# Sorting the 21-slot block inside the round instead of at its end, reading rows back later, and finishing the last three rounds side by side

## The chip, the core and the metric

The kernel runs on one core of a Trainium2 chip. The metric is the device time of one execution in microseconds (us); the number given for a kernel is the median of its timed runs. Engines are called by the profile's names: PE (TensorE matmuls), PEld (its weight loads), DVE (VectorE), ACT (ScalarE), POOL (GpSimd) and SP (SyncE). [...]

## What is computed

The input is 16 graphs of 1024 nodes with 64 features, an adjacency of 16 x 1024 x 1024 and a node mask. Four layers follow each other, each one `layernorm(x + layer(x))`. Layers 0 and 1 are dense message passing. Layers 2 and 3 are what the changed code does: for every node and feature, the values of the neighbours are sorted and weighted quantiles are taken, then a small MLP follows.

```python
adj_d = _dilate_adj(adj, mask)                        # thins out long neighbour lists
vals  = jnp.where(valid[..., None], x[:, None, :, :], big)
sv    = jnp.sort(vals, axis=2)                        # per node and feature, over neighbours
for tau, wt in zip((.25, .5, .75), (.25, .5, .25)):   # lo, hi: floor and ceil of tau * (m - 1)
    agg = agg + wt * (gather(lo) * (1.0 - frac) + gather(hi) * frac)
h = relu((x + agg) @ W1 + b1);  y = (h @ W2 + b2) * mask
```

## The kernel before

**Tiles and slots.** The 1024 nodes of a graph are ordered by the length of their neighbour list and cut into 8 blocks of 128 rows. A block is sorted as a dense list of a fixed number of slots, 64 features in each: `SIZES = (10, 11, 13, 14, 15, 17, 19, 21, 33)`. Blocks 0 to 6 (the "listed" classes t0 to t6, with 10 to 19 slots) have all their rows' neighbours fetched by POOL: one indirect DMA a slot and graph (line 378, tile `got_s`), from a table of the layer's features in DRAM. The last block is split in two halves of 64 rows; one graph's half needs up to 21 slots, the other's up to 33, and two graphs' halves are put side by side on the 128 partitions. So each pair of graphs has a block of class t7 (21 slots) and one of class t8 (33 slots). They aren't fetched: `fill` picks their values with one-hot matrices on PE (line 374, 24 matmuls for one slot of one graph, called a pick here), into PSUM tile `pgk`, and ACT copies them to SBUF tile `got` (line 780). The one-hots (`hot`) are made by DVE, every fourth by ACT.

**Rounds.** The 16 graphs are 8 pairs and there are two sorting layers, so 16 rounds (layer, pair), k0 to k15: (0,0), (0,1), (1,0), (0,2), (1,1), (0,3), ..., (0,7), (1,6), (1,7). `sort_round(k)` goes through t6, t5, ..., t0 for both graphs at once, then t7, then t8. `exchange` runs the min/max network of a class on DVE (49 instructions for t7, 66 for t8, 222 for t0 to t6); `weigh` multiplies the wanted slots on ACT and adds them on DVE. `finish` does the MLP and the layernorm, and POOL writes the rows by an indirect DMA (line 888): to the output, or to the table of the next layer, from which `read_back` loads them with an SP DMA (line 902) and splits them into three bf16 parts for `fill`.

**The ring.** `got_s` has `ROOM = 60` slots for both graphs of a round, the classes of a round need 99. `fetch` lets POOL go ahead as far as slots are free: t6, t5 and t4 of a round take slots 0 to 50, and t3 takes slots 0 to 13 again, so t3's gathers wait until t6 of their own round is sorted and weighed.

**The order of the work.** All instruction streams of DVE, ACT and PE are written out by generators that `Weave` runs by an estimated DVE clock: each `yield n` says that n us of DVE work should come before the generator goes on, and `catch_up` is called after each exchange instruction. So the preparation of later graphs (`features`, `lists`, `ordered`), `fill`, `weigh` and `finish` lie between the exchanges in an order fixed when the program is built. `weave.finish(gen)` and `weave.advance` write out a generator's rest at once.

The functions that the change touches are `fill` (line 762), `read_back` (line 897), `finish_round` (line 1018) and `sort_round` (line 1038). In `fill` the loop runs over the graphs, and within a graph over slots 1 to 32; `filled[layer]` of a graph is set when its 32 picks are out, and `read_back` of graph b waits for `filled[1]` of graph b - 2. At its end `sort_round` does this:

```python
        weave.finish(filling)
        for t in range(LISTED, NS):
            off = sum(SIZES[LISTED:t])
            got = tails[k][:, off : off + SIZES[t], :]
            other = s.lists.tile([P, WIDE, C], F32, name="other", bufs=1)
            exchange(t, (got, other[:, : SIZES[t], :]), cut)
            summed(t, got, None, (0, 1))
```

Of the kernel before, what the change touches and what calls it, by code (L numbers as in the profile page):

```python
# [12 lines left out]
F32 = mybir.dt.float32  # L13
# [8 lines left out]
P = 128  # L22
# [5 lines left out]
LISTED = 7  # L28
# [188 lines left out]
def adj_resnorm_kernel(ctx: ExitStack, tc: tile.TileContext, x, adj_t, nodemask, w01, b01, w02, b02,  # L217
# [49 lines left out]
    def halves_of(b):  # L267

        return (7, 8) if b % 2 == 0 else (8, 7)
# [100 lines left out]
    def pick(dst, hot, parts, first=True):  # L370

        for c in range(NT):
            for q in range(3):
                nc.tensor.matmul(dst, hot[:, c, :], parts[:, c, q, :], start=first and c + q == 0,  # L374
                                 stop=c == NT - 1 and q == 2)
# [386 lines left out]
    def fill(k):  # L762

        while k and (k - 1, NS - 1) not in free:
            yield 1
        size, short = SIZES[NS - 1], SIZES[NS - 2]
        got = tails[k] = s.lists.tile([P, short + size, C], F32, name="got", tag="got_l", bufs=1)
        layer, both = members(k)
        for m, b, e in both:
            while e.parts[layer] is None or e.xs[layer] is None or e.place is None or e.none is None:  # L770
                yield 1
            at = [(rows, (0, short)[plan - LISTED], SIZES[plan]) for rows, plan in zip((lower, upper), halves_of(b))]
            for rows, off, _ in at:
                nc.scalar.copy(got[rows, off, :], e.xs[layer][rows, NT - 1, :])
            waiting = None

            def empty():
                for rows, off, most in at:
                    if waiting[0] < most:
                        nc.scalar.copy(got[rows, off + waiting[0] : off + waiting[0] + 4, :], waiting[1][rows])  # L780

            for i in range(1, size):
                if i % 4 == 1:
                    first, pg = i, pgs[i // 4 % 2]
                if i % 4 == 1:

                    far = s.work.tile([P, NT, P], F16, name="far", bufs=1)
                    nc.scalar.activation(far, e.place, AF.Abs, bias=minus_k[:, i + 2 : i + 3])
                    by_act = s.lists.tile([P, NT, P], BF, name="hot", bufs=HOTS)
                    nc.scalar.activation(by_act, far, AF.Relu, bias=one_f, scale=-1.0)  # L790
                if i % 4 == 3:
                    hot = by_act
                else:
                    hot = s.lists.tile([P, NT, P], BF, name="hot", bufs=HOTS)
                    dve.tensor_scalar(hot, e.place, float(i), None, op0=ALU.is_equal)
                whole = i < LEAST[NS - 2]
                if not whole:
                    nc.tensor.matmul(pg[:, i - first, :], e.none,
                                     ident_b[: KW - 1, i - 1 : i].to_broadcast([KW - 1, C]), start=True, stop=False)
                pick(pg[:, i - first, :], hot, e.parts[layer], whole)  # L800
                yield 2.4
                if i % 4 == 2 and waiting:
                    empty()
                if i % 4 == 0:
                    waiting = first, pg
            yield 5
            empty()
            yield 0.5
            e.filled[layer] = True

    def weigh(k, t, got, agg, which, present):

# [84 lines left out]
    def read_back(b, e, src):  # L897

        while b >= 2 and not entries[b - 2].filled[1]:
            yield 2  # L900
        x3 = s.feat.tile([P, NT, C], F32, name="x3", bufs=1)
        nc.sync.dma_start(x3, src[:N, :].rearrange("(t p) c -> p t c", p=P))
        yield 60
        parts = s.feat.tile([P, NT, 3, C], BF, name="x3p", bufs=2)
        yield from split(x3, parts, x3)
        e.parts[1] = parts
# [40 lines left out]
    entries = [SimpleNamespace(near=None, taken=False, packed=False, listed=False, there=None, place=None, none=None,  # L947
                               wts=None, parts=[None, None], xs=[None, None], filled=[False, False], ends=None) for _ in range(B)]
    weave = Weave()
    tails = {}  # L950
    free, gots, room, holders = set(), [], [0], [None] * ROOM
    allowed, fetched = [1], [0, 0]
    order_of_rounds = [(0, 0), (0, 1)]
# [23 lines left out]
    def fetch(must=-1):  # L977

        moved = True
        while moved:  # L980
            moved = False
            for m in range(2):
                n = fetched[m]
                if n < len(tasks) and (m == 0 or n <= fetched[0]):
                    moved = fetch_one(n, m, must) or moved
# [32 lines left out]
    def finish_round(k, agg, sums):  # L1018
        for gen in sums:
            while weave.runs(gen):  # L1020
                yield 1
        layer, both = members(k)
        if k == len(order_of_rounds) - 1:
            for m, b, e in both:
                weave.add(finish(b, e, layer, agg[:, m], m == 1))
            return
        for m, b, e in both:
            yield from finish(b, e, layer, agg[:, m])

    def exchange(t, pair, view):  # L1030

        for is_max, d, v, i, j, to in usual[t]:
            dve.tensor_tensor(view(pair[to], v, d if is_max else 0), view(pair[i], v), view(pair[j], v, d),
                              op=ALU.max if is_max else ALU.min)
            weave.catch_up()
            fetch()

    def sort_round(k):

        if k >= 2:  # L1040
            weave.finish(rounds[k - 2])
        filling = weave.add(fill(k), 4.0, 0.7 if k < 3 else 1.0)
        agg = s.feat.tile([P, 2, NT, C], F32, name="agg")
        sums = []

        def summed(t, got, which, present):
            if len(sums) >= 2:
                weave.finish(sums[-2])
            sums.append(weave.add(weigh(k, t, got, agg, which, present)))
            weave.catch_up()  # L1050

        for n, (_, t, present) in enumerate(tasks):
            if tasks[n][0] != k:
                continue
            fetch(n)
            got = gots[n]
            which = slice(present[0], present[-1] + 1)
            count = len(present)
            other = s.lists.tile([P, WIDE, C], F32, name="other", bufs=1)
            other = other[:, : count * SIZES[t], :].rearrange("p (e s) c -> p e s c", e=count)  # L1060
            exchange(t, (got[:, which], other), cut_pair)
            summed(t, got, which, present)
        weave.finish(filling)
        for t in range(LISTED, NS):
            off = sum(SIZES[LISTED:t])
            got = tails[k][:, off : off + SIZES[t], :]
            other = s.lists.tile([P, WIDE, C], F32, name="other", bufs=1)
            exchange(t, (got, other[:, : SIZES[t], :]), cut)
            summed(t, got, None, (0, 1))
        if k:  # L1070
            weave.finish(rounds[k - 1])
        rounds.append(weave.add(finish_round(k, agg, sums)))
# [308 lines left out]
```

## Time and profile before

| | |
|---|---|
| timed runs | 7385.34, 7337.73, 7328.73 us; median 7337.73 us |
| the profiled execution | 5306.79 us, its span 5304.9 us |
| DVE busy | 4297.6 us, 81% of the span |
| POOL busy | 3464.7 us, 65% |
| PE busy | 3435.2 us, 65%; weight loads 2659.3 us, 50% |
| ACT busy | 2809.1 us, 53% |
| mean granted PE clock | 0.743 |
| POOL's indirect DMAs | 2944 gathers, 128 + 128 row writes |

The profiled execution took 2031 us less than the median of the timed runs; the page is of the profiled one. A busy share is a mean over the whole span, in which the first rounds, the middle and the last rounds have different limits. In a wait line the first number is the total, then how many times, then the longest. A wait is that of the engine named first[...]. DVE's groups are all recorded at line 211, a helper, so they are told apart by tiles.

### The profile page before, as it was taken

The numbers are of one execution on the slowest core, as the hardware profiler recorded it, in microseconds if no ns is written. First come the engines' busy times: TensorE is split into PE (matmuls) and PEld (weight loads), VectorE is DVE, ScalarE is ACT, GpSimd is POOL, SyncE is SP. The second block draws the span as 40 slices with busy tenths as digits, with TensorE's granted clock in tenths as the row PEclk, the third lists the DMA queues.
The fourth block names the chain that finished last, engine by engine and source line by source line (L and its number), as shares of the span: only waits on it lengthen the run. The fifth ranks groups of instructions, "written<-read, shape, count | busy, mean of one in ns | idle before, by whom it ended". The sixth has DMA issues, their size and how long they took to land. (4 is left out here: it accounts for less than half of the span.)

```text
span 5304.9 us, 109613 instructions
## 1 busy us (share of the span) xinstructions
PE 3435.2 (65%) x43576; PEld 2659.3 (50%) x43576; DVE 4297.6 (81%) x9266; ACT 2809.1 (53%) x6314; POOL 3464.7 (65%) x3296
## 2 busy tenths in 40 slices
PE   6878886385775776666776785777769563424152
PEld 5756555264554565555565563655547352324141
DVE  2577849698788989797997988798999999596775
ACT  3466465456564665737384563738475653334242
POOL 0336417757567776767767574776767777777771
PEclk7888787687877787868787786878887775555555
DMA  2212212222222222222212122222222111111110
GB/s 84 76 50 69 68 32 66 47 48 54 48 60 52 59 61 57 57 55 45 73 41 58 46 52 53 57 59 50 60 50 58 25 28 26 25 24 27 26 24 7
DMA packets 420617, 259.31 MB, mean 49 GB/s; under 512 B 106602, under 2 KB 368890, under 8 KB 420090
## 3 DMA queue, kind: packets, MB, share of 16 engines
q0 software_dynamic: 102400, 105.06, 10.4%
q1 hardware_dynamic: 317690, 147.12, 9.7%
q8 instruction: 343, 5.62, 0.5%
q14 instruction: 184, 1.51, 0.1%
HBM read 239.37 MB, written 12.59 MB: 47 GB/s over the span
## 5 line engine op out<-in xcount | busy, mean ns | idle before, releaser
L378 POOL DMA_INDIRECT got_s<-table,idx x2944 | 3170.9, 1077 | 1650.7 <-issue 604.9
L374 PEld LDWEIGHTS <-hot 128*128 128x128 bf16 x24576 | 972.2, 109 | 1011.9 <-DVE hot L211 696.7
L374 PE MATMUL pgk<-x3p,hot 128*128 128x64 bf16 x12288 | 544.0, 211 | 460.8 <-DVE hot L211 396.6
L211 DVE TENSOR_TENSOR other<-got_s 128x512 f32<-128x512 f32 (+9 forms) x850 | 508.7, 609 | 387.4 <-DMA got_s<-table,idx 352.9
L374 PE MATMUL pgk<-x2p,hot 128*128 128x64 bf16 x12288 | 525.5, 208 | 320.4 <-DVE hot L211 261.6
L780 ACT COPY got<-pgk 64x256 f32<-64x256 f32 x416 | 151.6, 365 | 675.8 <-PE pgk L374 670.3
L536 PE MATMUL pr<-steps,near 128*128 128x512 bf16 x1536 | 415.1, 431 | 131.6 <-ACT junk L542 84.6
L211 DVE TENSOR_TENSOR got_s<-got_s 128x128 f32<-128x128 f32 (+9 forms) x867 | 482.0, 560 | 17.8
L481 PE MATMUL pa<-x,adj_r 128*128 128x65 f32 x2048 | 391.3, 375 | 133.7 <-ACT x L404 58.6
L628 PE MATMUL pk<-near,order 128*128 128x512 f16 x2048 | 468.0, 382 | 4.5 <-DVE order L211 4.2
L829 ACT ACTIVATE got_s<-got_s,wts 128x64 f32<-128x64 f32 x1568 | 396.5, 335 | 135.1 <-DVE got_s L211 128.9
L481 PEld LDWEIGHTS pa<-x,adj_r 128*128 128x128 f32 x2048 | 380.6, 289 | 141.7 <-ACT x L404 60.5
L211 DVE TENSOR_TENSOR got_s<-other 128x512 f32<-128x512 f32 (+9 forms) x731 | 402.2, 563 | 7.5
L211 DVE TENSOR_SCALAR hot<-place 128x1024 bf16<-128x1024 f16 x768 | 329.8, 435 | 60.1 <-PE pgk L374 60.0
L536 PEld LDWEIGHTS <-near 128*128 128x128 f16 x1536 | 162.2, 109 | 353.0 <-issue 228.4
L211 DVE TENSOR_TENSOR other<-other 128x384 f32<-128x384 f32 (+10 forms) x617 | 324.0, 525 | 17.3
L211 DVE MAX8 best<-code 128x8 f16<-128x1024 f16 x240 | 293.9, 1225 | 48.1 <-ACT code L639 43.0
L628 PEld LDWEIGHTS <-order 128*128 128x128 bf16 x2048 | 194.0, 98 | 233.6 <-issue 10.6
L542 ACT ACTIVATE junk<-pr,nb_st 128x1024 f16<-128x1024 f32 x256 | 281.7, 1105 | 36.7 <-PE pr L536 35.9
L580 PE MATMUL pv<-minus_n,takes 128*128 128x128 bf16 x1024 | 212.5, 241 | 133.1 <-DVE takes L211 132.6
L790 ACT ACTIVATE hot<-far,one_f 128x1024 bf16<-128x1024 f16 x256 | 294.0, 1148 | 8.6
L450 PE MATMUL px<-adj_r,x_s 128*64 128x128 f32 x2048 | 287.9, 302 | 13.6 <-ACT node_in L453 9.2
(205 smaller groups left out, 6748.9 us busy)
## 6 DMA issues: line engine op xcount, KB each, us to landing
adj_r<-in_adj_dram SPq DMA_DIRECT2D x256, 512.0 KB
got_s<-table,idx POOLq DMA_INDIRECT x2944
x_s<-in_x_dram SPq DMA_DIRECT2D x16, 256.0 KB
table<-x SPq DMA_DIRECT2D x16, 256.0 KB
x<-table SPq DMA_DIRECT2D x16, 256.0 KB
table<-x3s,rows POOLq DMA_INDIRECT x128
out_dram<-agg,out_rows POOLq DMA_INDIRECT x128
table<-no_row SPq DMA_DIRECT2D x12, 0.2 KB
```

Source lines behind the costliest of these rows:

```text
L211: return call(*args, **kwargs)
L374: nc.tensor.matmul(dst, hot[:, c, :], parts[:, c, q, :], start=first and c + q == 0, stop=c == NT - 1 and q == 2)
L378: nc.gpsimd.indirect_dma_start(out=dst, out_offset=None, in_=tab, in_offset=bass.IndirectOffsetOnAxis(ap=rows, axis=0))
L450: nc.tensor.matmul(px[C:, q * P : (q + 1) * P], x_s[:, jt, :], adj[t][:, jt, :], start=jt == 0, stop=jt == NT - 1)
L481: nc.tensor.matmul(pa[:, q, :], adj[i][:, jt, :], x1[:, jt, :], start=jt == 0, stop=jt == NT - 1)
L536: nc.tensor.matmul(pr[:, h * HALF : (h + 1) * HALF], near[:, c, t * P : (t + 1) * P], steps[:, ONSET + h * HALF - c * P :][:, :HALF], star ...
L542: nc.scalar.activation(junk, prs[t - 1], AF.Sign, bias=lim[:, i, t - 1 : t], scale=-1.0, accum_out=cut_at[:, i, t - 1 : t])
L580: nc.tensor.matmul(pv[:, cols], takes[:, c, rows], minus_n, start=False, stop=False)
L628: nc.tensor.matmul(cols, order[:, c, t * P : (t + 1) * P], left(c, slice(h * G, (h + 1) * G)), start=c == 0, stop=c == NT - 1)
L780: nc.scalar.copy(got[rows, off + waiting[0] : off + waiting[0] + 4, :], waiting[1][rows])
L790: nc.scalar.activation(by_act, far, AF.Relu, bias=one_f, scale=-1.0)
L829: nc.scalar.activation(got[:, m, i, :], got[:, m, slot_id, :], AF.Copy, scale=e.wts[:, t, i : i + 1])
```

## The change

- `fill` keeps two tiles, `got_21` and `got_33`, where it had one of 54 slots, and turns its loops round: slots 1 to 20 of both graphs first, then slots 21 to 32 of both. A mark (k, 1) is set when the first part is out. `filled[layer]` of a graph is set at the end of its second part.
- `sort_round` sorts t7 ahead of t1 (after t2), once the mark (k, 1) is there; in the first round, k0, it stays at the end. t8 stays at the end.
- `read_back` of graphs 0 to 11 issues its SP DMA 60 us of DVE clock later, and the split comes 40 us after that, where it was 60 us after an immediate DMA. Graphs 12 to 15 stay as they were.
- `finish_round` lets the two graphs of rounds k13, k14 and k15 finish side by side (the second one in the buffers of `features` and in two other PSUM banks); before, only k15 did this, and the others finished one graph after the other.

```diff
 def fill(k):
-        size, short = SIZES[NS - 1], SIZES[NS - 2]
-        got = tails[k] = s.lists.tile([P, short + size, C], F32, name="got", tag="got_l", bufs=1)
+        middle, most = SIZES[NS - 2], SIZES[NS - 1]
+        ends = [s.lists.tile([P, size, C], F32, name="got", tag=f"got_{size}", bufs=1) for size in (middle, most)]
+        tails[k] = ends
         layer, both = members(k)
-        for m, b, e in both:
+        groups = 0
+        for low, high in ((1, middle), (middle, most)):
+            for m, b, e in both:
...
-            for i in range(1, size):
+                for i in range(low, high):
...
-            yield 5
-            empty()
-            yield 0.5
-            e.filled[layer] = True
+                yield 5
+                empty()
+                yield 0.5
+                if high == most:
+                    e.filled[layer] = True
+            filled.add((k, low))
 def read_back(b, e, src):
         while b >= 2 and not entries[b - 2].filled[1]:
             yield 2
+        if b < B - 4:
+            yield 60
         x3 = s.feat.tile([P, NT, C], F32, name="x3", bufs=1)
         nc.sync.dma_start(x3, src[:N, :].rearrange("(t p) c -> p t c", p=P))
-        yield 60
+        yield 60 if b >= B - 4 else 40
 def finish_round(k, agg, sums):
-        if k == len(order_of_rounds) - 1:
+        if k < order_of_rounds.index((0, B // 2 - 1)):
             for m, b, e in both:
-                weave.add(finish(b, e, layer, agg[:, m], m == 1))
-            return
-        for m, b, e in both:
-            yield from finish(b, e, layer, agg[:, m])
+                yield from finish(b, e, layer, agg[:, m])
+        else:
+            ends = [weave.add(finish(b, e, layer, agg[:, m], m == 1)) for m, b, e in both]
+            while any(weave.runs(gen) for gen in ends):
+                yield 1
 def sort_round(k):
+        def end(t):
+            got = tails[k][t - LISTED]
+            other = s.lists.tile([P, WIDE, C], F32, name="other", bufs=1)
+            exchange(t, (got, other[:, : SIZES[t], :]), cut)
+            summed(t, got, None, (0, 1))
+
         for n, (_, t, present) in enumerate(tasks):
...
+            if t == 1 and len(present) == 2:
+                while (k, 1) not in filled:
+                    weave.advance()
+                end(NS - 2)
             fetch(n)
...
         weave.finish(filling)
-        for t in range(LISTED, NS):
-            ...
+        if k == 0:
+            end(NS - 2)
+        end(NS - 1)
```

## The prediction

> **What bounds the kernel now.** I read the page first, then DVE's and POOL's waits, the timelines of round k7, SP's waits, and last the windows of the end.
>
> ```profile
> span 5304.9 us, 109613 instructions
> ...
> PE 3435.2 (65%) x43576; PEld 2659.3 (50%) x43576; DVE 4297.6 (81%) x9266; ACT 2809.1 (53%) x6314; POOL 3464.7 (65%) x3296
> ...
> DVE  2577849698788989797997988798999999596775
> ...
> POOL 0336417757567776767767574776767777777771
> ```
>
> DVE is the fullest engine, near nine tenths in the middle of the span. But a share doesn't say what it waits for. DVE's waits over the whole span, then (second fence) from 961 to 3745 us alone, which holds k1's t1 to k10's t1:
>
> ```profile
> DVE other L211 <- DMA got_s<-table,idx: 352.9, 28, 26.4
> DVE hot L211 <- PE pgk L374: 60.0, 28, 5.4
> ...
> DVE near L211 <- DMA adj_r<-in_adj_dram: 36.0, 7, 22.6
> ```
> ```profile
> DVE other L211 <- DMA got_s<-table,idx: 188.9, 14, 26.4
> ...
> DVE near L211 <- DMA adj_r<-in_adj_dram: 22.6, 1, 22.6
> ```
>
> One wait towers: exchanges whose gathered rows haven't landed. In the timeline of DVE in k7 it is one hole, between the end of t2 and the first exchange of t1; POOL's timeline of the same round shows why.
>
> ```profile
> 2787.02 0.42 DVE L211 TENSOR_TENSOR y_x<-pd,x_s 128x256 f32<-128x256 f32 x1
> 2812.33 0.56 DVE L211 TENSOR_TENSOR other<-got_s 128x384 f32<-128x384 f32 x1 [24.89 <-DMA got_s<-table,idx]
> ```
> ```profile
> 2642.45 1.10 POOL L378 DMA_INDIRECT got_s<-table,idx  x1 [0.30 <-issue]
> 2672.30 1.89 POOL L378 DMA_INDIRECT got_s<-table,idx  x1 [28.76 <-DVE other L211]
> ```
>
> POOL stops 28.76 us at the start of k7: counted out, the gather at 2672.30 is the first of t3, whose ring slots are t6's, and t6 isn't sorted because DVE was still in k6's t7 and t8. So there is a cycle: DVE sorts two blocks that need no gather (POOL fills the ring and stops), then consumes gathers faster than POOL brings them (DVE stops). Each has slack where the other works.
>
> [...] 24.89 us in which DVE starts nothing, though t7's block needs no gather. [...] I price an indirect DMA by its spacing, median 1.27 us. [...] Spacings under 3 us average 1.26 us where DVE spends under a fifth of the time in TENSOR_TENSOR and 1.43 us where over four fifths; so a filled hole slows POOL a little.
>
> **Part 1: t7 between t2 and t1.** I matched the exchange networks to DVE's records in order. The wait just ahead of t1 is, from k1 to k10: 26.4, 9.9, 11.8, 10.0, 14.7, 21.8, 24.9, 15.5, 18.0 and 8.2 us, together 161 us; the other 28 of the 188.9 us lie ahead of t2 (15.0 in k3, then three of about 4) and stay. t7 takes 19.3 us where nothing lies between its exchanges (k15), so it covers nearly every hole; in k1 and k7 a few us may be left.
>
> Is t7's block there? `fill` needs 40 picks before it, in place of 64. The 40th pick of a round ended before the end of t2 by 132 us in k1, 92 in k2, 32 in k4, 28 in k6, 14 in k7, 16 in k9, 10 in k10, but 7, 6 and 7 us in k13, k14 and k15. Two more flushes of the PSUM banks come in (5.5 us of DVE clock each, no instruction more). So it is just there; where it is late in k13 to k15, DVE would have waited for gathers.
>
> Does POOL keep up? A round has 184 gathers and 16 row writes, 200 x 1.36 us (mean spacing in unbroken runs) = 272 us; rounds k4 to k10 last 293 to 325 us. POOL's stops at t3 are 6.3, 19.5, 18.0, 28.8, 33.6, 49.6, 22.9 and 20.5 us in k4 to k11, about as large as the holes or larger, so a shorter round is paid from them.
>
> What is late next: DVE loses the pause in which PE and ACT caught up. In k7's window from 2642 to 2787 us DVE was busy 132.69 of 145 us; some 8% idle inside busy stretches will grow. I take 15% of the gain as given back, bounds 0 and 50%: 161 x 0.85 = 137 us (80 to 161). In k11 to k15 POOL has no stop over 3 us from 3910 us to 5135 us: it is the bound there, and moving DVE work gains nothing until the last gather is in.
>
> **Part 2: the SP read 60 us later.** SP's waits and, in k8, what one of them costs DVE:
>
> ```profile
> SPq L902 <- DMA table<-x3s,rows: 1289.3, 15, 431.5
> ```
> ```profile
> 3235.87 0.37 SPq L902 DMA_DIRECT2D x<-table  x1
> 3236.40 2.42 SPq L433 DMA_DIRECT2D adj_r<-in_adj_dram  x3
> ```
> ```profile
> 3241.16 0.69 DVE L211 TENSOR_SCALAR near<-adj_r 128x1024 f16<-128x1024 f32 x1 [22.57 <-DMA adj_r<-in_adj_dram]
> ```
>
> SP stood at the read because its rows were queued on POOL behind gathers; three adjacency loads stood behind it, and DVE waited 22.57 us for one. 60 us of DVE clock later the rows of most graphs have landed (the wait before this read was at most 51.9 us in k8). I take 22 us, of the 36.0 us that DVE lost to `adj_r` in all (0 to 36). Moved are one read a graph and, by 40 us, the split (three ACT copies, two DVE subtractions); its parts are used a round or more later: k1's read of graph 1 was split at 1035 us, `fill` of k2 began at 1096 us, so 40 us later is still in time. `filled` coming later for the first graph of a pair delays its read by some 90 us at most, with the same cover.
>
> **Part 3: the last rounds.** The end and the start of k15:
>
> ```profile
> 5144.00:5189.00 45.00, 33.01 (x514) 27.14 (x513) 34.84 (x78) 26.25 (x63) 14.84 (x14) 0.61 0.05 12
> 5189.00:5251.00 62.00, 1.21 (x35) 1.00 (x31) 54.73 (x127) 12.06 (x47) 8.46 (x8) 0.53 0.01 4
> 5251.00:5305.00 54.00, 18.29 (x56) 11.77 (x56) 9.36 (x20) 14.66 (x44) 15.49 (x16) 0.50 0.04 12
> ```
> ```profile
> 4992.27 0.56 DVE L211 TENSOR_TENSOR other<-got_s 128x384 f32<-128x384 f32 x1 [22.76 <-DMA got_s<-table,idx]
> ```
>
> (The columns are time, then PE, PEld, DVE, ACT, POOL busy.) t7 and t8 fill 5189 to 5251 us. With t7 ahead of t1: t2 ends at 5144, t7 19.3, t1 14.4, t0 13.7, so t0 ends near 5191, when `fill`'s last pick is in too (5190.2); t8 starts there instead of at 5208.3. That is 17 us; for the later flushes I take 15 (0 to 20). The wait at 4992.27 is for graph 15's gathers, behind its row writes, since graph 14 was finished first. Side by side the writes come near those of graph 14 (4857 us) instead of 4953 us, and this wait shrinks. But POOL was busy meanwhile with graph 14's gathers, so the same gathers remain and DVE waits for t3 and t2 instead: I take 0 for it (0 to 22). k13 and k14 are POOL's, 0; k15's own finish was side by side already.
>
> **Sum.** 137 + 22 + 15 = 174 us, of the profiled execution's own 5306.8 us: 5133 us. The timed median is 2031 us above the profiled execution and no view shows where these lie. I carry the microseconds over as they stand: 7337.7 - 174 = 7164 us. Were every interval stretched alike (7337.7 / 5306.8 = 1.383), the gain would be 241 us: 7097 us.
>
> **Rivals.** *A, POOL paces the timed runs.* If the 2031 us are the indirect DMAs' (2031 / 3200 = 0.63 us each), a round is POOL's at 200 x 2.0 = 400 us, POOL never stops at t3, and t7 merely waits in another place; only the end stays, about 20 us: 7318 us. For it: from 3910 us on POOL already sets the pace. Against: in k4 to k11 it stops once a round.
> *B, half is given back.* DVE runs into PE and ACT (fill copies, `takes`, `code`) after every hole that closes: 161 x 0.5 = 80, with 5 from the rest: 7253 us. For it: 60.0 us of `hot` waiting for PE already. Against: those waits are at most 5.4 us each.
> *C, slower: the mid-round sort waits for its block.* DVE is parked ahead of t7, and behind it stand the one-hots, the preparation of later graphs and the weighing, for which PE, ACT and POOL wait. If the 40th pick were out 20 us after t2 in each of k1 to k15, DVE would lose 300 us and save the 161: +139, less 37 of parts 2 and 3: 7440 us. It decides from when that pick is later than t2 by more than the hole it replaces, 11 us on average. For it: margins of 6 to 7 us in the last three rounds. Against: 10 to 132 us in the rounds before.
> That the move is void is excluded but for k0, where t7 stays at the end.
>
> **How the numbers follow.** Forecast 0.52, A 0.20, B 0.18, C 0.10. The forecast's own range is 7090 to 7240. The range over all: below, all bounds (161 + 36 + 42) stretched would give 7007, of which I allow 7050; above, A with little gained, 7335; C is left out. A difference of about 1% (73 us) is what a measurement of this kernel can tell from no change. Faster by over 1%: the forecast and two thirds of B, 0.64; within 1%: A and the rest of B, with a rest of C, 0.27; slower: 0.09.
>
> **What would show it.** Right: DVE's wait for `got_s` falls from 352.9 to below 200 us with no hole ahead of t1 in k1 to k10; POOL's stops at t3 shrink by 10 to 25 us each; SP's wait at the read falls below 500 us and DVE's for `adj_r` below 15; the stretch from t0's end to the span's end loses some 15 us. Wrong: a hole ahead of the mid-round sort, ended by the ACT copies of its block; POOL's stops unchanged; or a span near 5133 us with a median near 7318 us, which would be A.

## The result, and the profile after

The changed kernel takes 7303.97 us (median; 7279.55 to 7355.68), the kernel before 7331.09 us in the same comparison (7301.86 to 7385.34). The ratio is 0.9959, with a 95% interval of 0.9941 to 0.9977: the change takes off 0.4%, some 27 us, where 174 us (2.4%) were forecast. The profiled execution of the changed kernel took 7304.02 us, its span 7302.3 us.

Every execution of these kernels lies on one of two levels, near 5300 us or near 7350 us for the kernel before, and the profile of before from which the prediction was made (5306.79 us) is of the low one, while the timed runs that it stood beside, the recorded comparison and the profile after are of the high one; in the experiments, where each comparison was made on one chip, chips 4, 7 and 9 gave the low level and chip 15 the high one.

The page of the changed kernel, busy time by engine and then DVE's and POOL's slices:

```profile
span 7302.3 us, 109619 instructions
...
PE 3967.8 (54%) x43576; PEld 2889.7 (40%) x43576; DVE 4309.3 (59%) x9266; ACT 2805.3 (38%) x6312; POOL 3317.1 (45%) x3296
...
DVE  2546536567456566466574855658484765747475
...
POOL 0432235445363443536445454446446353765652
```

DVE has as much to do as before (4309.3 and 4297.6 us), but in a span that is 1997 us longer; no engine is full anywhere. DVE's waits over the span say what it lacks:

```profile
DVE hot L211 <- remote: 687.2, 74, 44.7
...
DVE hot L211 <- PE pgk L374: 187.3, 71, 16.8
...
DVE other L211 <- ACT got L784: 161.8, 7, 56.0
...
DVE near L211 <- DMA adj_r<-in_adj_dram: 13.2, 6, 5.5
```

The wait for gathered rows, 352.9 us in the profile before, is down to one of 0.7 us. In its place DVE waits for the one-hots' buffers to come free, that is for PE's picks (the name "remote" stands where the records name no releaser; all 74 of these waits are for a semaphore that only PE's instructions update). And the longest wait of PE's matmuls is for nothing that the trace shows:

```profile
PE pgk L374 <- issue: 850.4, 1103, 8.5
...
PE ordered_x L374 <- issue: 270.7, 204, 2.6
```

"Issue" is idle time for which the profile shows no semaphore, buffer or engine that was waited for. POOL, for its part, stands and waits for DVE:

```profile
POOL got_s L378 <- DVE other L211: 1108.9, 84, 99.7
```

Was the kernel before like this when it was timed? A second profile of it, taken on chip 15 at the high level (span 7353.6 us, first experiment below), says yes. DVE's and POOL's waits in it:

```profile
DVE hot L211 <- remote: 708.6, 81, 45.8
DVE hot L211 <- PE pgk L374: 392.3, 77, 33.5
...
DVE other L211 <- DMA got_s<-table,idx: 19.6, 3, 16.1
```
```profile
POOL got_s L378 <- DVE other L211: 1248.7, 77, 95.5
```

So 161 us of holes ahead of t1, on which the forecast rests, were not there in the timed runs: 16.1 us in k1 is all that is left ahead of t1 in k1 to k10. The place in k7 that the prediction showed with a hole of 24.89 us looks like this in the second profile (DVE's timeline):

```profile
3955.79 0.42 DVE L211 TENSOR_TENSOR y_x<-pd,x_s 128x256 f32<-128x256 f32 x1 [24.76 <-remote]
3956.13 0.55 DVE L211 TENSOR_TENSOR other<-got_s 128x384 f32<-128x384 f32 x1
```

They are the same two instructions. Here DVE lost its time one instruction earlier, on a matmul result (`pd`; the semaphore that it waited for is PE's), and the last gather of t1 had been issued at 3851.0 us, 105 us before.

What holds PE up is best seen in one stage that runs early and alike in all kernels: the 512-column matmuls of `ordered` at line 628. PE's timeline of the changed kernel at the low level (the run called after_again), and POOL's at the same time:

```profile
199.93 7.07 PE L628 MATMUL pk<-near,order 128*128 128x512 f16 x32
```
```profile
202.33 0.94 POOL L378 DMA_INDIRECT got_s<-table,idx  x1 [0.30 <-issue]
203.58 0.94 POOL L378 DMA_INDIRECT got_s<-table,idx  x1 [0.30 <-issue]
```

And the recorded profile after, the same code at the high level, PE and POOL:

```profile
201.81 0.59 PE L628 MATMUL pk<-near,order 128*128 128x512 f16 x2 [1.04 <-issue]
203.22 0.38 PE L628 MATMUL pk<-near,order 128*128 128x512 f16 x1 [0.82 <-issue]
204.63 1.01 PE L628 MATMUL pk<-near,order 128*128 128x512 f16 x2 [1.04 <-issue]
206.02 0.58 PE L628 MATMUL pk<-near,order 128*128 128x512 f16 x1 [0.38 <-issue]
```
```profile
202.66 0.94 POOL L378 DMA_INDIRECT got_s<-table,idx  x1 [0.30 <-issue]
203.90 0.94 POOL L378 DMA_INDIRECT got_s<-table,idx  x1 [0.30 <-issue]
```

POOL does the same in both, one indirect DMA every 1.25 us. At the low level PE runs 32 matmuls in one unbroken piece of 7.07 us. At the high level it gets one or two, then nothing for about 1 us, then one or two again, in a beat of some 1.4 us. Some fifteen microseconds earlier, as POOL's first gather began (186.22 us), 16 such matmuls still took 3.63 us in one piece:

```profile
186.09 3.63 PE L628 MATMUL pk<-near,order 128*128 128x512 f16 x16
```

Over whole traces, PE's gaps (neither a matmul nor a weight load) of over 250 ns that are put down to issue, split by whether POOL had an indirect DMA in hand at the gap's start (the time up to 0.4 us after one counted in):

```
                                  POOL busy with indirect DMAs     POOL not
before, low level (chip 7)              71 us    (14 gaps)           74 us
before, high level (chip 15)          1519 us  (2122 gaps)          204 us
after, low level (chip 4)               66 us    (12 gaps)           52 us
after, high level (recorded)          1526 us  (2074 gaps)          202 us
```

The first column grows by 1519 - 71 = 1448 us, where the prediction left 2031 us unexplained. The two can't simply be subtracted, since PE isn't always what the rest waits for; but in the chain of work that ended last, "issue" takes 20.7% of the kernel before on chip 15, some 1520 us. The same trace also shows what goes with the gaps: a pick of 24 matmuls takes 2.34 us on average where POOL has an indirect DMA in hand at its start and at its end, and 1.10 us where it has none at either. At the low level (before, chip 7) these are 1.06 and 1.05 us.

Two rivals can be looked for in these traces. The first is that PE's instructions come in more slowly. The packets of the trace's instruction queue (16 KB each; the kernel of experiment 6 has 110592 PE instructions more and 432 packets more, one for 256 instructions) take 1.09 us on average in the kernel before on chip 15 and 1.13 us on chip 7, no longer, and in the stretch shown above the gaps come after one or two matmuls. The second is that what POOL does to issue a gather, before the gather's packets move, holds PE up while it goes on. In the kernel before on chip 15 POOL stands for over 5 us 130 times. In the first 1.2 us after it starts again, one gap begins in 124 us of PE work, and no packet of the gathers has moved yet (the earliest comes after 1.55 us). In the first 1.2 us after its last DMA before such a stop, 107 gaps begin in 56 us of PE work, although POOL does nothing any more, and their rate is down to 10 in 107 us only in the fifth microsecond. The gaps follow the gathers' transfers, then, more than POOL's own work. That is a coincidence in time and not an experiment, and why the first microsecond stays nearly free of gaps isn't shown. SP's transfers alone don't bring them: away from POOL's indirect DMAs (5 us and more after one) gaps take 0.8% of PE's time while SP's packets move.

The stretch after t0 of k15, as windows of the kernel before on chip 15 and of the recorded profile after:

```profile
7224.70:7353.00 128.30, 31.61 (x300) 22.34 (x297) 71.58 (x163) 35.49 (x110) 23.99 (x24) 0.54 0.02 7
```
```profile
7200.00:7302.00 102.00, 22.83 (x130) 15.85 (x130) 47.49 (x99) 23.34 (x79) 15.49 (x16) 0.50 0.02 6
```

The stretch is 26 us shorter, since t7 has left it; k15 up to the end of t0, where t7 lies now, is 5 us longer (232.9 and 237.8 us).

### The profile page after: what moved, and what is told of

Same layout as the page of the kernel before. It is cut to its first block, busy times and chain, and to the rows that moved or that the text cites. A ratio compares the mean times of both kernels' runs of the same rounds, so it can differ in the third digit from the quotient of the medians.

```text
span 7302.3 us, 109619 instructions
## 1 busy us (share of the span) xinstructions
PE 3967.8 (54%) x43576; PEld 2889.7 (40%) x43576; DVE 4309.3 (59%) x9266; ACT 2805.3 (38%) x6312; POOL 3317.1 (45%) x3296
## 4 chain that ended last, share of the span: by engine, by line
PE 30%; DVE 22%; issue 21%; another core or an unknown queue 13%; ACT 12%; POOL 1%; DMA 0%; DVEq 0%; ACTq 0%; POOLq 0%
PE pgk L374 9%; DVE other L211 7%; PE pk L628 5%; DVE got_s L211 4%; DVE got L211 4%; PE px L450 3%; PE pr L536 3%; PE pa L481 2%; ACT got_s L835 2%; DVE best L211 2%; PE ordered_x L374 2%; ACT junk L542 1%; ACT dist L557 1%; ACT got L784 1%
## 5 line engine op out<-in xcount | busy, mean ns | idle before, releaser
L378 POOL DMA_INDIRECT got_s<-table,idx x2944 | 3029.0, 1029 | 3557.4 <-DVE other L211 1108.9
L374 PEld LDWEIGHTS <-hot 128*128 128x128 bf16 x24576 | 1096.2, 112 | 1999.6 <-issue 1608.7
L374 PE MATMUL pgk<-x3p,hot 128*128 128x64 bf16 x12288 | 654.4, 214 | 745.7 <-issue 423.5
L374 PE MATMUL pgk<-x2p,hot 128*128 128x64 bf16 x12288 | 659.7, 215 | 632.5 <-issue 426.9
L628 PE MATMUL pk<-near,order 128*128 128x512 f16 x2048 | 528.8, 408 | 83.4 <-issue 72.7
L536 PE MATMUL pr<-steps,near 128*128 128x512 bf16 x1536 | 444.2, 447 | 121.6 <-ACT junk L542 54.0
L481 PE MATMUL pa<-x,adj_r 128*128 128x65 f32 x2048 | 410.7, 386 | 109.0 <-ACT x L404 57.0
L450 PE MATMUL px<-adj_r,x_s 128*64 128x128 f32 x2048 | 325.8, 315 | 136.1 <-issue 122.4
L450 PEld LDWEIGHTS px<-adj_r,x_s 128*64 128x64 f32 x2048 | 273.5, 160 | 184.0 <-issue 163.1
L802 PE MATMUL pgk<-ident_b,none 32*128 32x64 bf16 x448 | 92.7, 207 | 420.7 <-ACT got L784 363.8
```

Of the source, the lines that this page charges most:

```text
L378: nc.gpsimd.indirect_dma_start(out=dst, out_offset=None, in_=tab, in_offset=bass.IndirectOffsetOnAxis(ap=rows, axis=0))
L450: nc.tensor.matmul(px[C:, q * P : (q + 1) * P], x_s[:, jt, :], adj[t][:, jt, :], start=jt == 0, stop=jt == NT - 1)
L481: nc.tensor.matmul(pa[:, q, :], adj[i][:, jt, :], x1[:, jt, :], start=jt == 0, stop=jt == NT - 1)
L536: nc.tensor.matmul(pr[:, h * HALF : (h + 1) * HALF], near[:, c, t * P : (t + 1) * P], steps[:, ONSET + h * HALF - c * P :][:, :HALF], star ...
L628: nc.tensor.matmul(cols, order[:, c, t * P : (t + 1) * P], left(c, slice(h * G, (h + 1) * G)), start=c == 0, stop=c == NT - 1)
L802: nc.tensor.matmul(pg[:, i - first, :], e.none, ident_b[: KW - 1, i - 1 : i].to_broadcast([KW - 1, C]), start=True, stop=False)
```

## The experiments

Ratios are to the kernel before on the same chip, in the same comparison.

**1. The kernel before once more, at both levels.** No edit.

> The unchanged kernel, for a second profile. Theory P (PE is starved): its profile lasts about 7300 us, not 5305; PE waits for nothing that the profile shows ('issue') for over 1000 us in all, nearly all of it while POOL issues gathers; and DVE's wait for gathered rows, 352.9 us in the first profile, is under 60 us, so that there is no hole ahead of t1 to fill. Theory Q (POOL paces the round, my rival A): the profile lasts as long, but the start-to-start spacing of POOL's gathers is near 1.9 us and DVE's wait for gathered rows is over 1000 us. Theory R (the first profile was typical, the time is lost outside the span): a span near 5300 us again.

> The unchanged kernel once more, for its profile beside the next three. Theory P: near 5300 us DVE waits some 360 us for gathered rows; near 7330 us (should this execution be of that kind) under 60 us, and PE has over 1000 us of 'issue' while POOL gathers.

On chip 7: 5297.68 us, ratio 0.9999 (0.9992 to 1.0007), span 5292.6 us; on chip 15: 7355.44 us beside a median of 7361.78 us for the other runs there. So profiling isn't what makes the low level: a profiled execution on chip 15 is as long as the timed ones. Of what was expected of before_again nothing came quite as put: the span is near 5300 us as in R, but so are the 20 timed runs, so no time lies outside the span. before_third came as P had it (19.6 us for gathered rows, 1519 us of issue gaps with POOL's indirect DMAs). DVE's first wait on chip 7 is that of the first profile:

```profile
DVE other L211 <- DMA got_s<-table,idx: 364.6, 30, 26.7
```

**2. The three parts one by one, low level (chip 7).** mid_only is the change without its edits of `read_back` and `finish_round`; the two others are the kernel before with one edit each.

```diff
 # read_only
+        if b < B - 4:
+            yield 60
         x3 = s.feat.tile([P, NT, C], F32, name="x3", bufs=1)
...
-        yield 60
+        yield 60 if b >= B - 4 else 40
 # side_only
-        if k == len(order_of_rounds) - 1:
+        if k < order_of_rounds.index((0, B // 2 - 1)):
... (and the rest of finish_round as in the change)
```

> The mid-round sort alone (two tiles, both graphs' slots 1 to 20 first, t7 ahead of t1); the read and the finish as before. P: no hole to fill, so the gain is that of the end alone, 0 to 20 us: 0.997 to 1.000 of before. Q: the same 15 to 20 us. My recorded step 1 at its recorded size: 137 us, 0.981.

> The later SP read alone. P: SP's wait at the read shrinks by hundreds of us, but DVE's wait for the adjacency is small beside its waits for PE and ACT: 0.998 to 1.002 of before. My recorded step 2: 22 us, 0.997.

> Rounds k13 and k14 finished side by side, all else as before. P: in the usual state PE limits the last rounds too, so the shorter chain of a finish (two graphs at once in place of one after the other) is worth 5 to 30 us where k15 waits for k13's rows: 0.996 to 1.000. My recorded step 3 gave the side-by-side part 0 us: 1.000.

Before took 5298.71 us there. mid_only: 5100.34 us, 0.9618 (0.9605 to 0.9631). read_only: 5294.68 us, 0.9988 (0.9980 to 0.9997). side_only: 5283.36 us, 0.9974 (0.9963 to 0.9984). mid_only does better than all that was expected of it (0.981 at best), read_only and side_only lie where P had them, and side_only gives what the prediction had put at nothing. The mid-round sort is nearly the whole change; DVE's wait for gathered rows has fallen by 212 us, and POOL's for DVE by 155 (before_again's first wait is shown above; POOL's was 263.3 us in it). Ahead of t1 in k1 to k10, the holes that were to be filled, 159.6 us in before_again, are 15.5 us in mid_only and 13.4 us in the whole change (experiment 3). DVE and POOL of mid_only:

```profile
DVE other L211 <- DMA got_s<-table,idx: 152.5, 16, 22.9
```
```profile
POOL got_s L378 <- DVE other L211: 108.2, 116, 14.8
```

Matched round by round with before_again, t6 of k1 starts 1 us earlier, of k4 48, of k7 99, of k10 184 and of k15 182 us earlier, so all of the gain comes in k1 to k10, as forecast, and none in k11 to k15. In read_only DVE's wait for `adj_r` fell from 37.2 to 20.8 us:

```profile
DVE near L211 <- DMA adj_r<-in_adj_dram: 20.8, 7, 6.4
```

In side_only k15 starts 15 us earlier than in before_again (4962.8 and 4978.0 us), k14 at the same time, since graph 15's gathers no longer stand behind its late row writes. But k15 gives most of that back, waiting for gathered rows as long as before (55.5 us in place of 57.4): its t0 ends only 4.3 us earlier (5159.1 and 5163.4). Some 9 us more come between t0 and t7: in before_again 13.4 us pass there, with one-hots and the finish of a graph of k14, for which DVE waits for PE:

```profile
5173.73 0.42 DVE L211 TENSOR_TENSOR y_m<-pd,b32r 128x256 f32<-128x256 f32 x1 [2.85 <-PE pd L878]
...
5176.78 0.48 DVE L211 TENSOR_TENSOR other<-got 128x320 f32<-128x320 f32 x1
```

In side_only that finish is out of the way by then, and t7 starts 4.3 us after t0's end.

**3. The whole change at the low level (chips 4 and 9).** No edit.

> The changed kernel, unaltered, against the kernel before on one chip. Before has by now run at about 5300 us (its two profiles, and 36 timed runs beside the first experiments) and at about 7330 us (the 20 timed runs beside the recorded result). Theory P (where PE issues at its full pace the change is worth what its parts are worth alone; where PE is starved of instructions while POOL gathers, almost nothing): if before takes near 5300 us here, the ratio is 0.9618 x 0.9988 x 0.9974 = 0.958, about 5077 us; if before takes near 7330 us, 0.996. Rival I (the parts hinder each other, which is why the whole gave 0.996): 0.98 or more although before takes near 5300 us.

> The changed kernel once more. Where before takes near 7350 us, its recorded ratio is 0.9959; where before takes near 5300 us, 0.9696. Theory S (it is the later read that takes the gain back where PE is starved, since without it the ratio was 0.979): again 0.990 to 0.998 near 7350 us. Rival X (the ratio 0.979 without the read is scatter of slow executions): whole and part lie within 0.5% of each other.

On chip 4: 5135.95 us, 0.9696 (0.9672 to 0.9720); on chip 9: 5137.49 us, 0.9692 (0.9675 to 0.9708). Its profiled execution on chip 4 took 5129.72 us; the prediction's sum for this number was 5133 us. But the whole is worse than mid_only alone (0.9618), so a part takes something back: the ratio is neither P's 0.958 nor rival I's 0.98 or more. The second run, meant for the high level, came to lie on the low one and repeats the first. DVE's and SP's waits of the whole change:

```profile
DVE other L211 <- DMA got_s<-table,idx: 197.5, 21, 21.0
```
```profile
SPq L910 <- DMA table<-x3s,rows: 1089.7, 13, 443.2
...
SPq L910 <- ACT x3p L418: 160.4, 4, 84.3
```

The last line is a read (line 910 here) that waits for the split of the read before it: `x3` has one buffer. In the version without the later read (mid_side_2, next experiment) this wait is 106.5 us; in both, 84.3 us of it is the last graph's read, behind which no adjacency load stands. Behind the other reads stand adjacency loads, and PE's waits for them, 3.3 us in mid_side_2, now are:

```profile
PE px L450 <- DMA adj_r<-in_adj_dram: 37.5, 4, 20.2
```

Two of the four make 34.0 us of it. The longer one, on SP, PE and DVE:

```profile
3566.58 0.37 SPq L910 DMA_DIRECT2D x<-table  x1
3567.04 9.88 SPq L433 DMA_DIRECT2D adj_r<-in_adj_dram  x4
```
```profile
3572.84 3.67 PE L450 MATMUL px<-adj_r,x_s 128*64 128x128 f32 x16 [20.24 <-DMA adj_r<-in_adj_dram]
```
```profile
3578.45 0.42 DVE L211 TENSOR_TENSOR y_m<-pd,b22r 128x256 f32<-128x256 f32 x1 [20.55 <-PE pd L884]
```

PE stands for a load that is queued behind the read, and DVE for PE. This read had waited 75.2 us for its rows, and the one before PE's other wait (13.7 us) 82.3 us; in mid_side_2 the same two reads waited 49.4 and 42.2 us. So the two reads that cost something stood for their rows, and not for the buffer.

**4. The change without the later read, at the low level and at the high one.**

```diff
-        if b < B - 4:
-            yield 60
         x3 = s.feat.tile([P, NT, C], F32, name="x3", bufs=1)
...
-        yield 60 if b >= B - 4 else 40
+        yield 60
```

> The change without its later SP read. Alone, the three parts gave 0.9618, 0.9988 and 0.9974; whole they gave 0.9696, some 35 us short of the product. Theory S (the later read is what hurts in company: with the mid-round sort, both graphs of a pair release their read later, the second read waits for the one x3 buffer, and adjacency loads stand behind it): 0.959 or less, better than the whole. Rival W (the side-by-side finish is what hurts): 0.967 to 0.972.

> The change without its later SP read. Theory S (the later read is what hurts in company): near 5300 us 0.957 to 0.962, better than the whole (0.9692 and 0.9696); near 7350 us again 0.972 to 0.986. Rival W (the side-by-side finish hurts): near 5300 us 0.967 to 0.972. Rival X (scatter): near 7350 us 0.990 or more.

Low level (chip 7): 5083.78 us beside 5297.36 us, 0.9595 (0.9582 to 0.9608), a full 1% better than the whole change, with intervals that lie apart. So the later read, worth 0.1% by itself, costs 1% beside the other two parts, as theory S had it; rival W is out. S's mechanism is only half right: adjacency loads do stand behind the read, but where PE had to wait for them the read waited for rows and not for `x3` (experiment 3). The two rounds in which they lie, k6 and k10, are 12 and 19 us longer than in this version, of the 41 us by which the whole change is later at the start of k11 (3712.4 and 3671.4 us). Why the rows are awaited longer beside the mid-round sort isn't shown. High level (chip 15): 7193.23 us beside 7361.78 us, 0.9790 (0.9722 to 0.9857). Its median is the lowest at both levels of the versions that compute the same values, though at the low one mid_only (0.9618, 0.9605 to 0.9631) is close. DVE's waits on chip 15:

```profile
DVE hot L211 <- remote: 517.4, 57, 47.4
DVE hot L211 <- PE pgk L374: 288.8, 76, 35.6
...
DVE other L211 <- ACT got L784: 166.3, 8, 36.6
```

The waits for one-hots fall from 708.6 + 392.3 us to 806.2, that is by 295, and 166 us come back as a wait for `got`, of which 118 us stand ahead of the mid-round sort and 49 ahead of t8. One reading, not tested, is that t7 in mid-round gives DVE something to do while PE catches up. There is a gain at the high level too, then, by another wait than the one forecast, and the whole change (0.9959, 0.9941 to 0.9977) doesn't keep it. That the later read is what loses it at this level as well follows from the two ratios, not from a pair of runs on one chip; and how it does so is open, since the waits for adjacency loads are small there and hardly larger than in this version (PE 6.9 and 1.1 us, DVE 13.2 and 13.3 us).

**5. Is PE the bound? Two matmuls a chunk for three, low level.** The picks leave out the lowest of the three bf16 parts.

```diff
-            for q in range(3):
+            for q in range(2):
... (and the last matmul of a sum is marked at q == 1)
```

> The kernel before with picks of two bf16 parts in place of three: 16 matmuls a slot in place of 24 (in the fill and in the ordering of the features), so 9216 matmuls and as many weight loads fewer; the third part, some 8 low bits of these values, is left out. P: near 5300 us PE is not the bound, and this gives 0.99 to 1.00; near 7330 us each PE instruction costs several hundred ns while POOL gathers, and it gives 0.85 to 0.95. Rival T (the slow executions are slow in DVE or in POOL): 0.99 to 1.00 there too.

> The changed kernel with picks of two bf16 parts (the third, some 8 low bits of these values, left out). P: near 5300 us as the changed kernel or up to 1% better; near 7330 us the gain of two parts, and a part of the change's own gain comes back with it: 0.80 to 0.93.

> The mid-round sort and the side-by-side finish without the later read, with picks of two bf16 parts (the third, some 8 low bits of these values, left out). Theory P near 7350 us: 18400 PE instructions fewer, of which under half fall beside POOL's gathers, so 0.85 to 0.95 of before, against 0.979 with three parts; near 5300 us 0.950 to 0.958. Rival T (slow in DVE or POOL): as with three parts.

Before: 5279.91 us, 0.9965 (0.9954 to 0.9977). With the whole change: 5106.81 us, 0.9632 (0.9607 to 0.9657); with experiment 4's version: 5060.18 us, 0.9553 (0.9536 to 0.9569). A third of the pick's matmuls is worth 0.35% before and 0.4 to 0.6% after, so PE hardly bounds the low level, before or after, as P had it. None of the three ran at the high level, so P's larger gains there, and rival T, are untested. What P supposed for that level, several hundred ns for each PE instruction, is too much by the traces: a pick with POOL's DMAs in hand takes 1.24 us longer than one without, some 50 ns for each of its 24 matmuls with its weight load.

**6. PE made late by hand, high level (chip 15).** Each pick is issued three times over.

```diff
-            for q in range(3):
+            for n in range(9):
... (part n % 3, and the last matmul of a sum is marked at n == 8)
```

> The kernel before with PE made the late engine by hand: each pick is issued three times over (72 matmuls a slot in place of 24, summed, so the picked values are tripled; this holds for the fill and the ordering of the features). Theory P: PE becomes the bound, some 2 ms of matmuls more, 6000 to 7500 us, DVE's wait for gathered rows falls from 364.6 to under 100 us and DVE waits for PE instead.

> The changed kernel with the same tripled picks. P: where PE is late there is no hole ahead of t1, and the change gives at most the end: 0.98 to 1.01 of heavy_before, where the two kernels differ by 0.9696 with picks issued once. Rival V (the mid-round sort helps whichever engine is late, since it fills any pause): 0.96 to 0.97 of heavy_before.

8990.63 us without the change and 8920.51 us with it, ratios 1.2208 (1.2129 to 1.2287) and 1.2132 (1.2050 to 1.2213); one against the other 0.992. The time is beyond P's 6000 to 7500 us, but DVE's wait for gathered rows is 17.8 us, under P's 100, and the ratio lies in P's 0.98 to 1.01: with PE late the change is worth little, as in the recorded comparison (0.996), and rival V (0.96 to 0.97) is out. The intervals of the two ratios overlap, so the 0.8% is not sure by itself. The runs also tell on the clock: the mean granted PE clock was 0.669 in the recorded profile and 0.753 in the same kernel's at the low level (after_again), but 0.745 in heavy_before, the longest run of all, and 0.700 in the profiled execution of two_parts, which took 5290.92 us. So a low clock doesn't go with the long level by itself.

**7. What POOL's pace costs, low level (chips 4, 9, 7).** The gathers become plain DMAs of the table's first 128 rows, from POOL, and then from SP. Theory P is here that what POOL does to issue an indirect DMA holds PE up at the high level, rival U that the bytes which the gathers move do.

```diff
-        nc.gpsimd.indirect_dma_start(out=dst, out_offset=None, in_=tab,
-                                     in_offset=bass.IndirectOffsetOnAxis(ap=rows, axis=0))
+        nc.gpsimd.dma_start(dst, tab[:P, :])     # pool_plain;  sp_rows: nc.sync.dma_start(...)
```

> The kernel before with each gather replaced by a plain DMA of 128 neighbouring rows from the same POOL queue (same bytes, same waits, other rows: the sorted values are not the neighbours' values). P: [...] near 7330 us this falls by over 500 us; near 5300 us it changes little unless the plain DMA's spacing on POOL differs from 1.27 us, in which case DVE's wait for gathered rows (364.6 us) goes with it. Rival U (starving by DMA traffic): near 7330 us nothing changes, since the bytes are the same.

> The gathers as plain DMAs of 128 neighbouring rows on the same queue (other rows than the neighbours'). Near 5300 us it gave 0.9365, and DVE's wait for gathered rows went. Theory P near 7350 us: [...] 0.75 to 0.9. Rival U (the bytes starve it): 0.97 to 1.00.

> The same plain row DMAs issued from SP's queue, so that POOL makes no gather at all (other rows than the neighbours'; SP's adjacency loads now stand behind the gathers' waits for ring slots). Theory P near 7350 us: PE's 'issue' falls from over 1500 us to under 300 us and the time to 5000 to 6000 us; near 5300 us: 0.93 to 1.00, DVE's wait for gathered rows gone, some of it given to waits for the adjacency. Rival U: near 7350 us, 0.97 to 1.00.

> The gathers as plain DMAs of neighbouring rows from SP's queue (other rows than the neighbours'). Near 5300 us 0.935, as before. Near 7350 us: theory P [...] 4950 to 6000 us, 0.67 to 0.82, with PE's 'issue' under 300 us; rival U (the gathers' bytes starve it) 0.97 to 1.00.

pool_plain: 4961.25 and 4955.22 us, 0.9365 (0.9340 to 0.9390) and 0.9351 (0.9335 to 0.9367). sp_rows: 4946.86 and 4945.68 us, 0.9350 (0.9325 to 0.9375) and 0.9341 (0.9326 to 0.9355). A plain DMA takes 548 ns of POOL on average (pool_plain), an indirect one 1077 ns (first profile of before). The wait for gathered rows is gone, and DVE's first wait (pool_plain) is

```profile
DVE hot L211 <- PE pgk L374: 72.0, 39, 5.1
```

So with plain DMAs of neighbouring rows in place of the indirect ones the kernel before takes 334 to 352 us less at the low level, and the mid-round sort takes off 198 without touching one DMA. The second runs of the two were meant for the high level, to see whether PE's gaps go with the indirect DMAs, but they came to lie on chips of the low level. That the gathers cause the gaps, and whether by what POOL does to issue them (P) or by the bytes that they move (U), was therefore tested by no run; the traces of the section above speak for the transfers (1 gap in 124 us of PE work before the packets move, 107 in 56 us after the last DMA).

## Why the prediction was wrong, by its own steps

**The step that failed: "I carry the microseconds over as they stand."** The prediction wrote down that 2031 us lay between the profiled execution and the timed runs and that no view showed where, and then took the profile's waits to be those of the timed runs. They were another regime. Of the 161 us of holes 16.1 us are there (second profile of before, k1), and the reading "DVE is the fullest engine" is of the low level alone: 81% there, 59% in the timed regime. For the low level the sum comes near: 174 us were forecast, and on chip 4 the medians differ by 159 us (5295.33 and 5135.95). That is luck. By its parts the mid-round sort gave 198 us where 152 were forecast, the side-by-side finish 15 where 0, and the later read took some 52 where it was to give 22; the errors cancel. The mechanism of the largest term, holes ahead of t1 that the sort of t7 fills, was right at that level.

**Part 1** was forecast at 137 us for the holes and 15 for the end. At the low level k1 to k10 gave 181 us (t6 of k11 starts at 3868.2 us in before_again and at 3686.4 us in mid_only). The 15% that was taken off for PE and ACT falling late didn't come: `hot` waiting for PE went from 55.1 to 40.4 us. In k1 to k10 the waits for gathered rows fell by 148 us, 144 of them ahead of t1; where the other 33 us come from isn't shown. At the end, the stretch from t0's end fell from 129.2 to 107.7 us, a little more than forecast, but t7 itself now lies inside k15 and isn't hidden there: from the start of t6 to the end of t0 k15 grew from 185.4 to 203.0 us. Net 4 us in place of 15. (The two profiled executions differ by 186 us, the medians by 198.) At the high level the stretch fell from 128.9 to 102.3 us and k15 before it grew by 5, net 22 of the 51.3 us between the two profiled spans there.

**The margins of k13 to k15.** The prediction saw the block ready 6 to 7 us ahead of the sort in these rounds, and held that a late block would cost nothing, since DVE would wait for gathers anyway. At the low level that nearly holds: mid_only waits 0.1 us ahead of t7 in k13 and k15, and not at all in k14, but 7.0, 4.0 and 3.2 us for `got` ahead of t8 in these rounds. At the high level it doesn't, as DVE's timeline of the changed kernel in k13 and k14 shows:

```profile
6471.32 0.49 DVE L211 TENSOR_TENSOR other<-got 128x320 f32<-128x320 f32 x1 [37.22 <-ACT got L784]
...
6839.49 0.49 DVE L211 TENSOR_TENSOR other<-got 128x320 f32<-128x320 f32 x1 [56.05 <-ACT got L784]
```

With 13.5 us in k15, and 23.9, 26.9 and 4.0 us ahead of t8 in these rounds, this is nearly the whole of the 161.8 us of `other` waiting for `got`. It is rival C's mechanism, in three rounds.

**Part 2** was mis-sized, in sign too. Forecast: 22 us, SP's wait at the read below 500 us, "with the same cover". Measured at the low level: about 6 us alone (0.12%), and some 52 us lost in company (5135.95 and 5083.78 us, on chips of equal level). SP's wait was 1307.7 us in before_again and 1213.7 us in read_only: moving the read by 60 us takes 60 us off few of these waits, the longest of which is 431.0 us. The term took the read's wait to shrink by the delay, and counted only what DVE would win by it; it left out that the adjacency loads behind the read are PE's too, and that such a load came only after a read that still waited (experiment 3: 20.24 us of PE for one load, 37.5 us in all).

**Part 3**, the side-by-side finishing, was put at 0 (0 to 22), because the same gathers would remain and DVE would wait for t3 and t2 instead. That reason held: of the 15 us by which k15 starts earlier 4.3 are left at the end of t0. Yet the part gave 15 us. What failed is "k13 and k14 are POOL's, 0": the finish of k14 reached into k15, between t0 and t7, where no gather is waited for, and 9 us came off there.

**The rivals.** A's number, 7318 us, is 14 us from the measured one, and its 20 us for the end are near the 22 measured. That is luck too, since its mechanism is refuted: it needed an indirect DMA every 2.0 us, and the spacing at the high level is 1.25 us, POOL standing 1108.9 us for DVE. What grew there is PE's idle time. B has nothing for it at the low level, where the closed holes gave nothing back. The signs that the prediction named came out so, at the low level: the wait for `got_s` below 200 us (197.5), right; no hole ahead of t1, nearly right (13.4 us left); POOL's stops smaller, right (263.3 to 151.6 us for the whole change); DVE's wait for `adj_r` below 15 us, right (13.0); SP's read below 500 us, wrong (1089.7); the end some 15 us shorter, right in that stretch (129.2 to 102.3 us) but not net of k15, which grew by 32.

## What to carry to other kernels

When the profiled execution and the timed runs differ by 38%, take the profile to be of another regime until one at the timed level is seen; a wait that towers in the one may be absent in the other, and no scaling of microseconds mends that. A move that fills a wait is worth what is waited for at the level at hand: here it was worth 3.8% where DVE waited for gathers, 2.1% (with the side-by-side finish) where it waited for PE, and 0.4% with the later read beside it. A transfer that is moved must be checked against what stands behind it in its queue and against every engine that waits for that, not only against the engine whose wait it was to shorten: here DVE's wait for `adj_r` was 13.0 us with the later read, and PE's at line 450 grew from 3.3 to 37.5 us.

## What the runs showed of the hardware that was not expected

- The same program takes 5295 to 5299 us on three chips and 7362 us on a fourth, with POOL's DMA spacing unchanged (median 1.26 and 1.25 us) and DVE's busy time within 0.3% (4295.7 and 4308.4 us). What differs most is gaps in PE's work that are put down to issue and come while POOL has indirect DMAs in hand (1519 us against 71). The pick's matmuls themselves take hardly longer: 213 to 215 ns in the second profile of the kernel before, 208 to 211 ns in the first. What makes the two levels stays open: chip 15 was used in one comparison only, so even whether it is the chip or the moment isn't shown.
- At the high level these gaps lag POOL: hardly any begins in the first 1.2 us after it starts again (1 in 124 us of PE work), and many begin in the 1.2 us after it has stopped (107 in 56 us).
- DVE and ACT show such gaps too at the high level, but few: 154 and 131 us in the kernel before on chip 15, 3 and 4 us on chip 7.
- A plain DMA of 128 rows issued by POOL or by SP gave the same time in this kernel to 0.2% (4955.22 and 4946.86 us, on one chip), so at the low level which queue issues them hardly matters once the indirect form is gone.
